# Attention on one core: the softmax's sums over keys moved from TensorE products to VectorE transposes and row sums

## The chip, the cores and the metric

The kernel runs on 1 core of one Trainium2 chip. The metric is the device time of that core in microseconds (us), the median of several runs.

## The reference

`x` holds 32 items of 512 rows by 512 features, `adj` is a 512x512 matrix of zeros and ones. Each item goes through two layers. The first is masked attention with 8 heads of 64 features, an addition of the input and a normalization of the rows; the second is a graph convolution, again with an addition and a normalization.

```python
q = (x @ Wq + bq).reshape(b, n, H, HD)      # k, v in the same way
scores = einsum('bihd,bjhd->bhij', q, k) / sqrt(HD) + mask   # mask: -1e9 where adj == 0
weights = softmax(scores, axis=-1)
x = layernorm(x + einsum('bhij,bjhd->bihd', weights, v).reshape(b, n, H*HD))
deg = adj.sum(axis=1)
norm_adj = adj * deg**-0.5 * deg**-0.5 (rows, columns)
x = layernorm(x + norm_adj @ (x @ weight) + bias)
```

What matters here is the denominator of the softmax: for each item, head and query the sum over 512 keys of exp(score).

## The kernel before, in words

**Layout.** Scores are made transposed: keys on the 128 partitions (4 tiles of keys), queries along the free dimension. One block is two heads of one item; there are 4 blocks an item (`ORDER` is 0, 2, 1, 3) and 128 in all (`blocks`). The exponentials of a block are four tiles `e` of 128x1024, one for each tile of keys, with the two heads side by side.

**The sums.** GpSimd adds the four `e` tiles of a block up into one tile `acc` (`accumulate`; its pool has 2 buffers). Then 128 keys on partitions are left to be summed. `sums(b, c)` does that on TensorE: four products with a 128x32 selector `sel`, one for each head of two blocks, into the four column groups of one PSUM tile. The result goes to `sT` by a copy on ScalarE (c = 0) or an addition on VectorE (c = 1). `finish(b).inverse` turns `sT` with four 128x128 transposes on TensorE, so that queries are on partitions, and takes reciprocals into `inv`. `add` multiplies the attention's result `yT` by `inv`.

**The order of the work is written out by hand.** Every engine takes its instructions in program order (`InOrder` pins it); no planner moves anything. The loop over k has one step for a block. In step k: what is left of the pending additions to `acc` is issued, then come `scores` for the first two key tiles of block k, `values` (the product with V) for block k-1, on every even k one call of `sums`, then `scores` for the last two key tiles. After that comes a share of "side" work: projections of the next item and the second half of the item before, with short pieces on other engines woven in (`beside`). `put_off` (`more`) issues one pending addition to `acc` on GpSimd.

For items 1 to 29 the four steps of an item are always alike. They are called here A (k mod 4 = 1), B (2), C (3) and D (0, the next item's first block). A share has 8 pieces of TensorE work of 1.7 to 1.9 us each:

- A: v0 to v6, the seven products for the next item's values (Strassen's scheme, `values_of`), and k0, the first of the keys and queries. `inverse` comes behind v5, `add` behind v6 and k0.
- B: k1 to k6, l0, l1 (keys and queries); the statistics, roots and `norm` of the first layer come between.
- C: l2, l3, l4, the four products `first` of the convolution, l5.
- D: l6 and the seven products `second` of the convolution.

**Buffers.** All these pieces, `sums` and `inverse` take PSUM tiles from the pool `ps_mm`, which has 3 buffers in turn: a piece starts only when the piece three before it has been read out. Scores have a pool of their own, `ps_sc`, with 2.

**The value pieces.** In `seven`, the piece v3 makes `u2` with `middle` (two additions: the product, then the bias `bv_r`), and v4 is read out by two VectorE instructions of which the first reads `u2`.

**judge** (three small VectorE instructions) checks that the inverses are in a safe range; it stands in B's share behind the last `split`.

Of the kernel before, what the change touches and what calls it, by code (L numbers as in the profile page):

```python
# [9 lines left out]
F32 = mybir.dt.float32  # L10
# [4 lines left out]
ALU = mybir.AluOpType  # L15
AX = mybir.AxisListType

P = 128
H = 8
# [30 lines left out]
def unshifted(  # L50
# [29 lines left out]
    B, N, D = x.shape  # L80
    NT = N // P
# [3 lines left out]
    tensor, vector, scalar, gpsimd = (InOrder(tc, e) for e in (nc.tensor, nc.vector, nc.scalar, nc.gpsimd))  # L85

    consts = ctx.enter_context(tc.tile_pool(name="consts", bufs=1))
    acts = ctx.enter_context(tc.tile_pool(name="acts", bufs=2))
    work = ctx.enter_context(tc.tile_pool(name="work", bufs=2))
    small = ctx.enter_context(tc.tile_pool(name="small", bufs=3))  # L90
# [10 lines left out]
    HALF = N // 2  # L101
# [77 lines left out]
    bv_r = load_row(bv, "bv_r", nc.scalar)  # L179
# [21 lines left out]
    gpsimd.memset(sel, 0.0)  # L201
    for c in range(2):
        gpsimd.memset(sel[:, c, c : c + 1], 1.0)
    FINE = consts.tile([P, B], F32, name="fine")
    maskT = consts.tile([P, NT, N], U8, name="maskT")
    adjT = consts.tile([P, NT, N], F32R, name="adjT")
# [74 lines left out]
    def values_of(b):  # L281


        def multiply(p, i, j):
            for r in range(2):
                for u in range(2):
                    tensor.matmul(
                        p[:, r, :], XT[:, j, u, ts(r, P)], wv[:, i, u, :],
                        start=u == 0, stop=u == 1,
                    )  # L290

        def first(e1, p):
            V[b] = acts.tile([P, NT, D], F32, name="v")
            vector.tensor_add(e1, p, bv_r[:, None, :HALF].to_broadcast([P, 2, HALF]))

        def middle(u2, u1, p):
            vector.tensor_add(u2, u1, p)
            vector.tensor_add(u2, u2, bv_r[:, None, HALF:].to_broadcast([P, 2, HALF]))

        def out(i, j):  # L300
            return V[b][:, 2 * j : 2 * j + 2, ts(i, HALF)]

        return seven(multiply, first, middle, out)
# [70 lines left out]
    def values(s):  # L374
# [27 lines left out]
        for q in range(4):  # L402
# [3 lines left out]
                yb[32 * q : 32 * (q + 1)],  # L406
            )

    def sums(b, c):


        p = ps_mm.tile([P, N], F32, name="mm")
        for q in range(4):
            parts = ACC[b, ORDER[2 * c + q // 2]]
            for k, a in enumerate(parts):
                tensor.matmul(
                    p[32 * q : 32 * (q + 1), :], sel[:, c, :], a[:, q % 2, :],
                    start=k == 0, stop=k == len(parts) - 1,
                )
        if c == 0:  # L420
            SM[b] = work.tile([P, N], F32, name="sT", bufs=1)
            if b < B - 1:
                scalar.copy(SM[b], p)
            else:
                vector.tensor_scalar(SM[b], p, 1e-36, None, op0=ALU.max)
        else:
            vector.scalar_tensor_tensor(SM[b], p, 1e-36, SM[b], op0=ALU.max, op1=ALU.add)

# [21 lines left out]
    def finish(b):  # L450


        t = {}

        def inverse(cs):
            sT = SM[b]
            p = ps_mm.tile([P, NT, 2, 2, 32], F32, name="mm")
            for i in range(NT):
                tensor.transpose(p[:, i].rearrange("p a k r -> p (a k r)"), sT[:, ts(i, P)], ident)
            if cs[0] == 0:  # L460
                t["inv"] = small.tile([P, NT, H], F32, name="inv")
            inv = t["inv"].rearrange("p i (a c k) -> p i a c k", a=2, c=2)
            for c in cs:
                vector.reciprocal(inv[:, :, :, c], p[:, :, :, :, c])

        def judge():

            inv = t["inv"].rearrange("p i h -> p (i h)")
            low = small.tile([P, NT * H], F32, name="low")
            vector.tensor_scalar(low, inv, INV_LOW, None, op0=ALU.is_gt)  # L470
            vector.scalar_tensor_tensor(low, inv, INV_HIGH, low, op0=ALU.is_lt, op1=ALU.mult)
            vector.tensor_reduce(FINE[:, b : b + 1], low, AX.X, ALU.add)

        def add(i):
            y = YT[b][:, i, :]
            vector.tensor_mul(
                y.rearrange("p (h d) -> p h d", h=H), y.rearrange("p (h d) -> p h d", h=H),
                t["inv"][:, i, :, None].to_broadcast([P, H, HD]),
            )
            gpsimd.tensor_add(y, y, R[b][i])  # L480

        def add_pair(i, g):

            y, r = YT[b][:, i, :], R[b][i]
            for h in (2 * g, 2 * g + 1):
                at = slice(h * HD, (h + 1) * HD)
                vector.scalar_tensor_tensor(
                    y[:, at], y[:, at], t["inv"][:, i, h : h + 1], r[:, at], op0=ALU.mult, op1=ALU.add
                )

        def measure(i):
            if i == 0:
                t["mv"] = small.tile([P, NT, 2], F32, name="mv")
            statistics(YT[b][:, i, :], t["mv"][:, i, :])

        def root(i=0, k=NT):
            rstd, add = roots(t["mv"][:, i : i + k], None)
            for n in range(k):
                t["rstd", i + n], t["add", i + n] = rstd[:, n : n + 1], add[:, n : n + 1]

        def norm(i):
            if i == 0:
                if b < B - 1:
                    HI[b], LO[b] = (acts.tile([P, NT, D], F32R, name=k, bufs=1) for k in ("hi", "lo"))
                    LO[b] = [LO[b][:, k, :] for k in range(NT)]
                else:
                    HI[b] = acts.tile([P, NT, D], F32R, name="hi2", tag="v")
                    lo = [acts.tile([P, 2, D], F32R, name="lo2", tag="kq", bufs=5) for _ in range(2)]
                    LO[b] = [lo[k // 2][:, k % 2, :] for k in range(NT)]
            x1 = YT[b][:, i, :]  # L510
            rstd, add = t["rstd", i], t["add", i]
            if b == B - 1 and i % 2:
                vector.tensor_scalar(x1, x1, rstd, add, op0=ALU.mult, op1=ALU.add)
            else:
                scalar.activation(x1, x1, AF.Identity, bias=add, scale=rstd)

            scalar.activation(HI[b][:, i, :], x1, AF.Copy, scale=dis[:, i : i + 1])

        def split(i):
            x1 = YT[b][:, i, :]  # L520
            vector.scalar_tensor_tensor(
                LO[b][i], x1, dis[:, i : i + 1], HI[b][:, i, :], op0=ALU.mult, op1=ALU.subtract
            )
            gpsimd.tensor_add(x1, x1, b1_r)

        def grow(i):
            x1 = YT[b][:, i, :]
            scalar.activation(x1, x1, AF.Copy, scale=rdeg[:, i : i + 1])

        def block(f):  # L530
            return [(0, f, (i,)) for i in range(NT)]

        return dict(
            early=[(0.6, inverse, ((0,),))], late=[(0.6, inverse, ((1,),))],
            pairs=[[(0, add_pair, (i, g)) for i in range(NT)] for g in ORDER],
            halves=[(0, root, (0, 2)), (0, root, (2, 2))],
            inverse=[(0.6, inverse, ((0, 1),))], add=block(add), measure=block(measure), root=[(0, root, ())],
            judge=[(0, judge, ())], norm=block(norm), split=block(split), grow=block(grow),
        )

# [156 lines left out]
    def cut(pieces, counts):  # L697

        lists = [[]]
        left = list(counts)  # L700
        for piece in pieces:
            if piece[0] > 1:
                if not left[0]:
                    left.pop(0)
                    lists.append([])
                left[0] -= 1
            lists[-1].append(piece)
        return lists
# [10 lines left out]
    S = len(blocks)  # L719
# [20 lines left out]
    for k in range(S + 1):  # L740
        b, at = divmod(k, G)
        if at == 1:
# [8 lines left out]
            if b == 0:  # L751
                w1_parts = [(0, weigh_part, (w1, gpsimd, i)) for i in range(4)]
                side = main[:7] + [(0, degrees, ())] + weave(w1_parts, main[7:]) + turn0 + kq[5:] + turn1
                shares = cut(side, (6, 5, 5, 5))
            elif b < B - 1:
                f, c = finish(b - 1), convolve(b - 1)
                norm, split, grow = f["norm"], f["split"], f["grow"]
# [6 lines left out]
                    5: rest[5:6] + f["inverse"], 6: rest[6:] + add[:2], 7: add[2:],  # L764
                    8: measure[:2] + put_off, 9: measure[2:], 10: f["root"] + put_off, 11: norm[:1],
                    12: norm[1:2] + split[:1], 13: norm[2:3] + split[1:2], 14: norm[3:] + split[2:3],
                    15: split[3:] + f["judge"], 16: put_off + grow[:2], 17: put_off + grow[2:], 18: turn0,
                }
                side = sum(([piece] + beside.get(i, []) for i, piece in enumerate(main)), [])
                side += c["first"] + c["parts"] + kq[5:] + turn1[:1]  # L770
# [26 lines left out]
            load_residual(B - 1)  # L797
        if k < S:
            scores((*blocks[k], 0))
        if k:  # L800
            values((*blocks[k - 1], 0))
            if k == S:
                sums(B - 1, 1)
            values((*blocks[k - 1], 1))
            if k % 2 == 0 and k < S:
                sums(blocks[k - 1][0], (k - 1) % G // 2)
        if k < S:
            accumulate((*blocks[k], 0))
# [324 lines left out]
```

## Time and profile before

| | |
|---|---|
| time, median of 3 runs | 2931.66 us (2931.45 to 2931.84) |
| span of the profiled execution | 2929.5 us, granted TensorE clock 0.995 |
| busy TensorE (PE) | 2874.0 us |
| busy VectorE (DVE) | 2081.8 us |
| busy GpSimd (POOL) | 1813.3 us |
| busy ScalarE (ACT) | 1059.1 us |
| chain of waits, by engine | PE 74%, DVE 16%, ACT 6% |
| products with `sel` on `acc` | 504 matmul records, 68.0 us busy |
| transposes of `sT` | 132 records, 19.9 us busy |
| `acc` additions on POOL | 374 of 128x1024, mean 2.36 to 2.41 us |

A matmul in float32 leaves several records. Busy times of an engine count overlapping instructions once. The profile's names follow the program's: `acc`, `sT`, `inv`, `u` for `u2`, `mm` for a tile of `ps_mm`, `sc` for one of `ps_sc`. Since every instruction is issued through the helper `InOrder`, all have its line (L44), and groups are told apart by tiles.

### The profile page before, as it was taken

The numbers are of one execution on the slowest core, as the hardware profiler recorded it, in microseconds if no ns is written. First come the engines' busy times: TensorE is split into PE (matmuls) and PEld (weight loads), VectorE is DVE, ScalarE is ACT, GpSimd is POOL, SyncE is SP. The second block draws the span as 40 slices with busy tenths as digits, with TensorE's granted clock in tenths as the row PEclk, the third lists the DMA queues.
The fourth block names the chain that finished last, engine by engine and source line by source line (L and its number), as shares of the span: only waits on it lengthen the run. The fifth ranks groups of instructions, "written<-read, shape, count | busy, mean of one in ns | idle before, by whom it ended". The sixth has DMA issues, their size and how long they took to land.

```text
span 2929.5 us, 35536 instructions
## 1 busy us (share of the span) xinstructions
PE 2874.0 (98%) x12966; PEld 1885.9 (64%) x12966; DVE 2081.8 (71%) x2926; ACT 1059.1 (36%) x1343; POOL 1813.3 (62%) x1139
## 2 busy tenths in 40 slices
PE   7999999999999999999999999999999999999997
PEld 5666666666666666666666666666666666666655
DVE  6677766677666777666776667776677766677677
ACT  1233333343333433333433334333333333343343
POOL 2566666656666666666666666666666666656665
PEclk9999999999999999999999999999999999999998
DMA  5111122112221121211122211122211122112211
GB/s 130 33 26 47 47 58 51 38 39 51 54 54 41 39 51 47 57 41 40 47 50 55 55 40 36 49 53 54 44 40 47 47 58 54 40 35 49 54 36 52
DMA packets 383401, 142.42 MB, mean 49 GB/s; under 512 B 280049, under 2 KB 349681, under 8 KB 383217
## 3 DMA queue, kind: packets, MB, share of 16 engines
q1 hardware_dynamic: 380720, 138.35, 19.8%
q10 hardware_dynamic: 2496, 1.70, 0.3%
q8 instruction: 104, 1.70, 0.2%
q14 instruction: 81, 0.66, 0.1%
HBM read 72.88 MB, written 33.55 MB: 36 GB/s over the span
## 4 chain that ended last, share of the span: by engine, by line
PE 74%; DVE 16%; ACT 6%; issue 2%; POOL 1%; DMA 0%; SPq 0%; DVEq 0%; POOLq 0%
PE mm L44 47%; PE sc L44 15%; PE av L44 12%; DVE u L44 3%; ACT yT L44 3%; DVE e L44 3%; DVE st L44 3%; ACT hi L44 2%; DVE lo L44 2%; DVE low L44 2%; POOL rstd L44 1%; ACT e L44 1%; DVE mv L44 1%; DVE kq L44 1%; DVE v L44 1%
## 5 line engine op out<-in xcount | busy, mean ns | idle before, releaser
L44 ACT ACTIVATE e<-e 128x1024 f32<-128x1024 f32 x512 | 540.6, 1057 | 1095.1 <-DVE e L44 1076.3
L44 DVE SCALAR_TENSOR_TENSOR e<-sc,maskT 128x1024 f32<-128x1024 f32 x512 | 600.3, 1213 | 83.1 <-PE sc L44 82.7
L44 POOL TENSOR_TENSOR acc<-acc,e 128x1024 f32<-128x1024 f32 x248 | 597.4, 2409 | 64.2 <-ACT e L44 54.4
L44 POOL TENSOR_TENSOR acc<-e 128x1024 f32<-128x1024 f32 x126 | 296.9, 2356 | 382.5 <-ACT e L44 271.4
L44 PE MATMUL sc<-kq 64*128 64x512 f32 x2048 | 518.9, 620 | 14.5 <-DVE e L44 14.5
L44 PE MATMUL mm<-xT,wk 128*128 128x256 f32 x1792 | 469.8, 385 | 1.0 <-DVE off L44 1.0
L44 PE MATMUL av<-e,v 128*64 128x512 f32 x2048 | 467.9, 599 | 0.0
L44 PE MATMUL mm<-xT,wq 128*128 128x256 f32 x1792 | 459.9, 379 | 0.0
L44 PE MATMUL mm<-wv,xT 128*128 128x256 f32 x1792 | 407.2, 385 | 18.2 <-DVE xT L44 11.7
L44 PEld LDWEIGHTS mm<-xT,wk 128*128 128x128 f32 x1792 | 332.7, 190 | 113.4 <-issue 69.7
L44 PEld LDWEIGHTS mm<-wv,xT 128*128 128x128 f32 x1792 | 338.3, 192 | 93.2 <-issue 24.3
L44 PEld LDWEIGHTS mm<-xT,wq 128*128 128x128 f32 x1792 | 340.9, 190 | 45.6
L44 PEld LDWEIGHTS sc<-kq 64*128 64x128 f32 x2048 | 174.2, 186 | 297.9 <-issue 171.9
L44 PEld LDWEIGHTS av<-e,v 128*64 128x64 f32 x2048 | 135.5, 136 | 316.2 <-issue 315.4
L44 DVE TENSOR_TENSOR kq<-u,mm 128x512 f32<-128x512 f32 x128 | 88.0, 688 | 238.0 <-PE mm L44 237.9
L44 POOL TENSOR_TENSOR yT<-yT,xr 128x512 f32<-128x512 f32 x124 | 193.6, 1590 | 80.5 <-DVE yT L44 80.5
L44 POOL TENSOR_TENSOR rstd<-ve,minus_half 128x4 f32<-128x4 f32 (+1 forms) x66 | 66.2, 1003 | 259.3 <-DVE nmu L44 259.3
L44 PE MATMUL mm<-w,zT 128*128 128x256 f32 x992 | 224.6, 379 | 0.0
L44 POOL TENSOR_TENSOR yT<-yT,b_r 128x512 f32<-128x512 f32 x124 | 171.2, 1391 | 56.4 <-DVE lo L44 56.4
L44 PEld LDWEIGHTS mm<-w,zT 128*128 128x128 f32 x992 | 188.4, 190 | 26.8 <-issue 1.5
L44 PE MATMUL mm<-adjT,hi 128*128 128x512 f32 x496 | 203.7, 411 | 0.0
L44 PE MATMUL mm<-adjT,lo 128*128 128x512 f32 x496 | 198.3, 400 | 5.2 <-DVE lo L44 5.2
(124 smaller groups left out, 3178.6 us busy)
## 6 DMA issues: line engine op xcount, KB each, us to landing
x<-in_x_dram SPq DMA_DIRECT2D x256, 128.0 KB, 2.9
out_dram<-y SPq DMA_DIRECT2D x127, 256.0 KB, 2.1
xr<-in_x_dram SPq DMA_DIRECT2D x124, 256.0 KB, 3.5
yT<-yb SPq DMA_DIRECT2D x496, 64.0 KB, 2.5
wv<-in_L_gnn_Wv_dram ACTq DMA_DIRECT2D x8, 128.0 KB, 4.5
wk<-in_L_gnn_Wk_dram SPq DMA_DIRECT2D x8, 128.0 KB, 4.3
wq<-in_L_gnn_Wq_dram SPq DMA_DIRECT2D x8, 128.0 KB, 4.5
yT<-in_adj_dram SPq DMA_DIRECT2D x1, 1024.0 KB, 6.6
```

The lines of the kernel that those rows point to most:

```text
L44: return self.tc.keep_in_program_order(op(*args, **kwargs))
```

## The change

For all items but the last, `fold(b, g)` takes the place of `sums`. It stands in step k behind the first pair of scores and ahead of `values`, for block k-1. It transposes `acc` in place on VectorE in blocks of 32x32 (one 128x1024 instruction), and sums each row over groups of 32 (one instruction, 128x1024 to 128x32) into a tile `folded` that gathers all 8 heads of the item. What is left is to add up, for each of 32 rows, the four groups of 32 partitions: `inverse_all` does it with one product of `folded` (128x128) with a constant `spread`, four small VectorE instructions that clamp and reorder the result, and one reciprocal.

Three more edits go along. The addition of `bv_r` to `u2` in the value pieces moves from VectorE to GpSimd. `judge` moves from B's share to C's, behind l4 and a transpose of x. For the first item, two calls of `more` are put into each share, so that `acc` is complete before `fold` wants it. The last item keeps `sums`, with `sT` in an old weight's buffer.

```diff
+    spread = consts.tile([P, 4, 32], F32, name="spread")
+    vector.tensor_reduce(spread[:, 0], ident.rearrange("p (q r) -> p r q", r=32), AX.X, ALU.add)
+    for q in range(1, 4):
+        gpsimd.tensor_copy(spread[:, q], spread[:, 0])
...
         def middle(u2, u1, p):
             vector.tensor_add(u2, u1, p)
-            vector.tensor_add(u2, u2, bv_r[:, None, HALF:].to_broadcast([P, 2, HALF]))
+            gpsimd.tensor_add(u2, u2, bv_r[:, None, HALF:].to_broadcast([P, 2, HALF]))
...
+    def fold(b, g):
+        a = ACC.pop((b, g))[0]
+        if g == ORDER[0]:
+            SM[b] = small.tile([P, H, N // 32], F32, name="folded")
+        vector.transpose(a.rearrange("p k n -> p (k n)"), a.rearrange("p k n -> p (k n)"))
+        vector.tensor_reduce(
+            SM[b][:, 2 * g : 2 * g + 2].rearrange("p k t -> p (k t)"),
+            a.rearrange("p k (t s) -> p (k t) s", s=32), AX.X, ALU.add,
+        )
...
         if c == 0:
-            SM[b] = work.tile([P, N], F32, name="sT", bufs=1)
-            if b < B - 1:
-                scalar.copy(SM[b], p)
-            else:
-                vector.tensor_scalar(SM[b], p, 1e-36, None, op0=ALU.max)
+            SM[b] = wq[:, 6].rearrange("p u n -> p (u n)")
+            vector.tensor_scalar(SM[b], p, 1e-36, None, op0=ALU.max)
...
+        def inverse_all():
+            p = ps_mm.tile([P, H, NT, 4], F32, name="mm")
+            tensor.matmul(
+                p.rearrange("p h i l -> p (h i l)"), spread.rearrange("p q r -> p (q r)"),
+                SM[b].rearrange("p h t -> p (h t)"), start=True, stop=True,
+            )
+            t["inv"] = small.tile([P, NT, H], F32, name="inv")
+            for l in range(4):
+                at = slice(32 * l, 32 * (l + 1))
+                vector.tensor_scalar(
+                    t["inv"][at].rearrange("p i h -> p h i"), p[at, :, :, l], 1e-36, None, op0=ALU.max
+                )
+            vector.reciprocal(t["inv"], t["inv"])
...
-            inverse=[(0.6, inverse, ((0, 1),))], add=block(add), measure=block(measure), root=[(0, root, ())],
+            inverse=[(0.6, inverse_all, ())], add=block(add), measure=block(measure), root=[(0, root, ())],
...
                 shares = cut(side, (6, 5, 5, 5))
+                for share in shares:
+                    share[1:1] = [(0, more, ())]
+                    share[4:4] = [(0, more, ())]
...
-                    15: split[3:] + f["judge"], 16: put_off + grow[:2], 17: put_off + grow[2:], 18: turn0,
+                    15: split[3:], 16: put_off + grow[:2], 17: put_off + grow[2:], 18: turn0 + f["judge"],
...
             scores((*blocks[k], 0))
+        if k and blocks[k - 1][0] < B - 1:
+            fold(*blocks[k - 1])
         if k:
             values((*blocks[k - 1], 0))
...
-            if k % 2 == 0 and k < S:
+            if k == S - 2:
                 sums(blocks[k - 1][0], (k - 1) % G // 2)
```

## The prediction, made before the changed kernel ran

> **What bounds the kernel now.** First the busy times of the page:
>
> ```profile
> PE 2874.0 (98%) x12966; PEld 1885.9 (64%) x12966; DVE 2081.8 (71%) x2926; ACT 1059.1 (36%) x1343; POOL 1813.3 (62%) x1139
> ```
>
> TensorE (PE) is busy for all but 55 of 2929.5 us, so what leaves PE shortens the kernel, unless a wait takes its place. Next, the busy times by step for one item (A, B, C, D):
>
> ```profile
> 1392.60:1414.88 22.28, 22.11 (x102) 14.94 (x101) 17.53 (x29) 7.16 (x8) 11.49 (x9) 1.00 0.33 102
> 1414.88:1437.30 22.42, 22.42 (x105) 14.68 (x104) 19.63 (x29) 10.62 (x16) 15.89 (x11) 1.00 0.08 12
> 1437.30:1460.01 22.71, 22.33 (x98) 14.38 (x97) 13.16 (x17) 10.49 (x15) 12.67 (x8) 1.00 0.18 35
> 1460.01:1482.43 22.42, 22.42 (x105) 14.68 (x104) 13.57 (x17) 4.81 (x5) 16.46 (x11) 1.00 0.19 40
> ```
>
> After the length come PE, weight loads, VectorE (DVE), ScalarE (ACT), GpSimd (POOL). An item takes 89.83 us. DVE has 2.8 us to spare in B, 4.8 in A, 9.6 in C, 8.9 in D. The timeline of PE shows what goes and the two places where PE already waits for DVE:
>
> ```profile
> 1410.48 0.60 PE L44 MATMUL mm<-ident,sT 128*128 128x128 f32 x4
> 1411.26 1.96 PE L44 MATMUL mm<-wv,xT 128*128 128x256 f32 x8 [0.17 <-DVE e L44]
> ...
> 1420.38 1.06 PE L44 MATMUL mm<-acc,sel 128*32 128x512 f32 x8
> 1421.37 1.99 PE L44 MATMUL sc<-kq 64*128 64x512 f32 x8
> ...
> 1443.25 2.26 PE L44 MATMUL sc<-kq 64*128 64x512 f32 x8 [0.38 <-DVE e L44]
> ```
>
> One call of sums holds PE for 1421.37 - 1420.38 = 0.99 us; the four transposes with the wait behind them for 1411.26 - 1410.48 = 0.78. That first wait is v6's, for the buffer of v4. The timeline of all engines shows its cause:
>
> ```profile
> 1405.40 0.16 DVE L44 TENSOR_SCALAR nmu<-mv 128x4 f32<-128x4 f32 x1
> ...
> 1405.56 1.02 POOL L44 TENSOR_TENSOR rstd<-ve,minus_half 128x4 f32<-128x4 f32 x1 [4.92 <-DVE nmu L44]
> ...
> 1406.80 5.14 POOL L44 TENSOR_TENSOR acc<-acc,e 128x1024 f32<-128x1024 f32 x2
> ...
> 1407.23 0.69 DVE L44 TENSOR_TENSOR u<-e,mm 128x512 f32<-128x512 f32 x1 [1.04 <-PE mm L44]
> ...
> 1407.95 1.77 DVE L44 TENSOR_TENSOR u<-u,bv_r 128x512 f32<-128x512 f32 x1
> 1409.82 0.69 DVE L44 TENSOR_TENSOR v<-u,mm 128x512 f32<-128x512 f32 x1
> ...
> 1410.43 0.68 DVE L44 TENSOR_TENSOR e<-e,mm 128x512 f32<-128x512 f32 x1
> ```
>
> v4's buffer is free when the last of these ends (1411.11). Last, the tiles view for durations (min/median/max in ns):
>
> ```profile
> L44 DVE STREAM_TRANSPOSE xT<-x x64: 1235/1239/1246, 8.3 to 2728.5; 128x1024 f32<-128x1024 f32 x64
> ...
> L44 DVE TENSOR_TENSOR u<-u,bv_r x32: 694/1770/2018, 26.5 to 2755.2; 128x512 f32<-128x512 f32 x32
> ```
>
> **What the skill says.** The Trainium skill, "SBUF — State Buffer", Who interferes with whom: a DVE instruction with two SBUF inputs and a GpSimd one that reads SBUF exclude each other for a whole instruction; one SBUF input or a row reduction doesn't contend. The trace agrees: u<-u,bv_r takes 694 ns at least and 1770 in the median beside acc additions, while the transposes of x stay within 11 ns. "VectorE: DVE Perf Modes", The perf-mode tier table, gives row reductions one element a cycle; the trace has 686 ns for 512 elements and 2280 for 2048. "TensorE: Matmul & The Clock Gate", Part 3, says that small products in different parts of the array overlap; the trace agrees: sums' four 512-column products take 0.99 us, so less goes than their count suggests.
>
> **The change part by part.** Per steady item, in offsets from the start of a step.
>
> PE: two calls of sums go (-1.98 us). The four transposes become one product of 128 columns: half of a 256-column one (8 records in 1.73 us make 4 products, 0.43 each), so 0.22; without any wait that is 0.78 - 0.22 = -0.56. Over 62 calls of sums and 31 inverses: 61.4 + 17.4 = 79 us, the most that can be won.
>
> DVE: each fold is a transpose (1.24) and a reduction of 1024 elements, 1.22 between the two rows above; the second reads the first, so 2.45 with the gap. Four an item: +9.8 us; off go one sT addition (0.69) and u+bv (1.77), and inverse_all takes some 0.9 in place of 0.36. The sT copy on ACT (0.57) goes too. DVE then has about 71.7 us of work in 87.3 of PE. The sum fits; where it stands decides.
>
> A: the first score readouts end at 4.45. Fold runs to 6.9, transposing av to 7.6, the second score readouts to 9.95 (before 9.04). Gaps of 1.17, 0.34, 0.42 and 0.22 us swallow most of it, and nmu ends at 13.21 instead of 12.96. u2's product is only ready at 14.6, so u2 ends at 15.3 as before. But now the bias is POOL's, and POOL takes its queue in order: rstd and add from 13.2 to 14.5, one acc addition to 16.85, and only then u2+bv, 1.28 us (the median of yT<-yT,b_r on POOL is 1276 ns, its maximum 1727), to 18.13. Behind this wait DVE holds both readouts of v4, which end at 19.5, and v6 starts at 19.65. PE is free for it at 18.1: a wait of 1.5 us. A is 19.65 - 18.66 = 1.0 us longer than before, 23.25.
>
> B: DVE enters as late as before (add ends at 3.6). Score readouts to 5.9, fold to 8.35, av to 9.0, score readouts to 11.3 (before 10.1), k1's readout to 11.95, then statistics and readouts without a gap: k2's is done at 14.1, k3's at 16.5, k4's at 17.9. PE has no sums now and reaches k6 at 16.17, which needs k3's buffer: 0.5 us of wait. B takes 22.42 - 0.99 + 0.5 = 21.93.
>
> C: the last split ends 0.75 later against B's start, and C begins 0.5 earlier: at 4.4 instead of 3.14. judge (1.6 us) is gone from there, so score readouts start at 4.35 instead of 4.68, and most of the 0.38 wait and of a second one inside that row (2.26 instead of 1.99) goes: -0.35, so 22.35. Fold then delays l2's readout to 12.6; the piece that needs its buffer starts at 12.9. judge, behind the transpose of x, lies beside the convolution's products, where DVE waited 6.7 us.
>
> D: -0.99, so 21.43; fold lies in the 2.0 us in which DVE waited for av, and the rest in later gaps.
>
> Sum: 23.25 + 21.93 + 22.35 + 21.43 = 88.96 against 89.83, so -0.9 an item, over 30 items -27. The first item: two sums less (-2), but in step 1 fold waits for two acc additions, which in this trace end at 77.4 on POOL; DVE then does the av transpose and the second score readouts at about 83, and the values' buffers hold PE for about 6 us. Together +4. spread is made while DVE and POOL wait for the first loads (8.3 and 11.0 us): nothing. The tile of sT for the last item changes its place only: nothing. No DMA moves.
>
> Total -23 us on the span of 2929.5; the other runs are within 0.4 us of one another and their median is 2.2 above the span, so 2909 us.
>
> Unknown costs, both ends. Fold: at the least 2.25 (two rows back to back without the gap), at the most 3.5 (if it waited for a POOL addition as u+bv does, +1.05). POOL's u2+bv: 1.26 to 1.73. inverse_all's small ones: 0.16 to 0.25 each, hidden until v6's readout at 21.6. fold's wait for acc: nothing after item 0, since the second addition of a block ends 5 us or more before the next step's fold. I take the medians.
>
> **The rivals.** (1) The main case: PE's gain is mostly given back as waits in A and B. (2) The waits don't come: POOL reaches u2+bv before the acc addition, and B's queue is shorter than reckoned. Then it is the 79 less 4 to 8: 2856 to 2864 us. For it: POOL is at 62%. Against it: the order on POOL is fixed, acc ahead of u2. (3) Slower: fold costs more than its rows. Every us on it delays A by one (through nmu, rstd, acc, u2), B by one (k6) and C by about half: 2.5 an item. The gain of 0.9 is gone from a fold of 2.8 us on; at 3.5 it is 88.96 + 2.6 = 91.6, over 30 items +53, +57 with item 0, so 2989. Against it: the even durations of the transposes of x. For it: B has nearly no slack, and an in-place transpose and 32 short sums in one instruction stand nowhere in this trace. (4) It does as it says but the waits eat all: within 6 us.
>
> **How the numbers follow.** 0.2% is 5.9 us, about what a measurement of this kernel can tell. Main case 0.55, 2882 to 2936, most of it faster; rival 2 0.18; rival 3 0.22; rival 4 0.05. Faster 0.55 x 0.85 + 0.18 = 0.65, same 0.055 + 0.05 = 0.11, slower 0.24. The range takes in rival 2 and the beginning of rival 3: 2860 to 2945.
>
> **What would show it right or wrong.** In the profile after, v6 waits about 1.5 us for DVE with v<-u,mm ended by POOL u; k6 waits about 0.5 for DVE; C's second scores wait less than 0.38; the fold pair takes 2.45 us; an item takes about 88.96 us and A is the one step that grew. If A shrinks, rival 2 holds; if fold takes over 2.8 us, rival 3.

## The result, and the profile after

The changed kernel takes 2891.85 us, the median of 4 runs (2891.36 to 2893.16), against 2931.55 for the kernel before on the same chip: a ratio of 0.9865, 95% interval 0.9848 to 0.9882, or 39.7 us less. The span of the profiled execution went from 2929.5 to 2890.0 us.

The busy times of the page after, to be held against the same line of before:

```profile
PE 2813.2 (97%) x12408; PEld 1867.5 (65%) x12408; DVE 2292.3 (79%) x3205; ACT 1041.4 (36%) x1312; POOL 1844.5 (64%) x1174
```

TensorE lost 61 us of busy time, VectorE got 210 and GpSimd 31 more. PE's unused time grew from 55 to 77 us: about a third of the busy time taken off PE came back as unused time. The four steps of one item (after the length: PE, weight loads, VectorE, ScalarE, GpSimd; then the granted clock) show where:

```profile
1287.90:1310.79 22.89, 21.88 (x99) 14.81 (x99) 18.65 (x33) 7.16 (x8) 12.33 (x10) 1.00 0.32 99
1310.79:1332.53 21.74, 21.69 (x97) 14.43 (x96) 20.46 (x30) 8.91 (x12) 15.29 (x10) 1.00 0.09 13
1332.53:1354.85 22.32, 22.32 (x98) 14.37 (x97) 16.36 (x20) 11.62 (x17) 13.03 (x9) 1.00 0.17 36
1354.85:1376.28 21.43, 21.43 (x98) 14.51 (x97) 15.16 (x18) 4.81 (x5) 16.80 (x11) 1.00 0.21 41
```

A is the one step that grew, by 0.61 us, and there PE is 1.01 us less busy than the step is long. D lost its 0.99 us of sums and nothing else. Items 2 to 29 repeat this within 0.1 us (in item 1, A took 22.52). The timeline of PE after has the places at which it waits (a bracket at the end of a row is the idle time before it and what ended it):

```profile
1305.78 0.39 PE L44 MATMUL mm<-folded,spread 128*128 128x128 f32 x2
1307.17 1.97 PE L44 MATMUL mm<-wv,xT 128*128 128x256 f32 x8 [1.01 <-DVE e L44]
...
1326.08 1.03 PE L44 MATMUL mm<-xT,wq 128*128 128x256 f32 x4
1327.16 1.13 PE L44 MATMUL mm<-xT,wk 128*128 128x256 f32 x4
...
1338.09 2.26 PE L44 MATMUL sc<-kq 64*128 64x512 f32 x8
```

v6 starts 1.01 us after PE was free. In B, k6 (the row at 1327.16) comes 1.08 us behind the row before it where its neighbours come after 0.86 or 0.87, so it is held for 0.2 though no bracket says so (a matmul's end is modelled). C's second scores have lost their bracket of 0.38; the row is still 2.26 us long, so the short wait inside it stayed. The timeline of GpSimd after shows why v6 waits,

```profile
1300.86 1.02 POOL L44 TENSOR_TENSOR rstd<-ve,minus_half 128x4 f32<-128x4 f32 x1 [4.92 <-DVE nmu L44]
1301.95 0.20 POOL L44 TENSOR_TENSOR add<-nmu,rstd 128x4 f32<-128x4 f32 x1
1302.11 2.37 POOL L44 TENSOR_TENSOR acc<-acc,e 128x1024 f32<-128x1024 f32 x1
1304.43 1.27 POOL L44 TENSOR_TENSOR u<-u,bv_r 128x512 f32<-128x512 f32 x1
1305.66 2.35 POOL L44 TENSOR_TENSOR acc<-acc,e 128x1024 f32<-128x1024 f32 x1
```

and that of VectorE after shows fold in its place and the wait that came with it:

```profile
1292.27 1.24 DVE L44 STREAM_TRANSPOSE acc<-acc 128x1024 f32<-128x1024 f32 x1
1293.54 1.22 DVE L44 TENSOR_REDUCE folded<-acc 128x32 f32<-128x1024 f32 x1
1294.67 0.71 DVE L44 STREAM_TRANSPOSE yb<-av 128x512 f32<-128x512 f32 x1
...
1302.53 0.69 DVE L44 TENSOR_TENSOR u<-e,mm 128x512 f32<-128x512 f32 x1 [1.04 <-PE mm L44]
1305.74 0.69 DVE L44 TENSOR_TENSOR v<-u,mm 128x512 f32<-128x512 f32 x1 [2.52 <-POOL u L44]
```

u2 is there at 1303.2, but its bias waits until 1304.43 behind rstd and an acc addition. VectorE sits for 2.52 us, in every item: the list of waits has "DVE v <- POOL u" with 75.9 us in 31 times.

The last place is step 1, once, in the timeline of all engines after:

```profile
76.46 1.25 DVE L44 STREAM_TRANSPOSE acc<-acc 128x1024 f32<-128x1024 f32 x1 [7.87 <-POOL acc L44]
...
82.57 8.08 PE L44 MATMUL mm<-wv,xT 128*128 128x256 f32 x24 [5.31 <-DVE e L44]
```

The first fold waits 7.87 us for acc, and PE then waits 5.31 us for a buffer. PE's 24 records behind that wait take 8.08 us; the 24 ahead of it take 5.45. The busy times of the stretch from 81.14 us on show why, in the granted clock of 0.50:

```profile
81.14:87.97 6.83, 5.40 (x13) 4.36 (x14) 3.34 (x5) 1.76 (x2) 5.56 (x3) 0.50 0.27 37
```

So step 1, which grew from 18.66 to 26.46 us, lost 5.3 us to the wait and some 2.5 to the clock behind it.

### The profile page after: what moved, and what is told of

Same layout as the page of the kernel before. It is cut to its first block, busy times and chain, and to the rows that moved or that the text cites. A ratio compares the mean times of both kernels' runs of the same rounds, so it can differ in the third digit from the quotient of the medians.

```text
span 2890.0 us, 34431 instructions
## 1 busy us (share of the span) xinstructions
PE 2813.2 (97%) x12408; PEld 1867.5 (65%) x12408; DVE 2292.3 (79%) x3205; ACT 1041.4 (36%) x1312; POOL 1844.5 (64%) x1174
## 4 chain that ended last, share of the span: by engine, by line
PE 81%; DVE 11%; POOL 3%; ACT 2%; issue 1%; DMA 0%; SPq 0%; DVEq 0%; POOLq 0%
PE mm L44 49%; PE sc L44 17%; PE av L44 16%; DVE e L44 3%; DVE st L44 2%; ACT y L44 2%; DVE v L44 1%; POOL u L44 1%; POOL rstd L44 1%; DVE mv L44 1%; DVE u L44 1%; DVE yb L44 0%; DVE kq L44 0%; DMA x<-in_x_dram 0%; DVE lo L44 0%
## 5 line engine op out<-in xcount | busy, mean ns | idle before, releaser
L44 POOL TENSOR_TENSOR acc<-acc,e 128x1024 f32<-128x1024 f32 x248 | 588.5, 2373 | 187.3 <-ACT e L44 182.5
```

The lines of the kernel that those rows point to most:

```text
L44: return self.tc.keep_in_program_order(op(*args, **kwargs))
```

## The experiments

Two theories stood against each other. "Places": PE has lost time at a few places only, each set by the order of one queue (v6 behind GpSimd's queue in A, k6 behind VectorE's in B, step 1). "Load": VectorE's 210 us of new work hold PE up wherever they stand. The table has what every run gave; the steps are medians over items 1 to 29 of each trace, from the first scores of a step to those of the next, and the times medians.

| kernel | A | B | C | D | item | time | ratio to before (95% interval) |
|---|---|---|---|---|---|---|---|
| before | 22.28 | 22.43 | 22.69 | 22.43 | 89.81 | 2931.6 | |
| forecast | 23.25 | 21.93 | 22.35 | 21.43 | 88.96 | 2909 | |
| changed | 22.90 | 21.74 | 22.31 | 21.43 | 88.38 | 2891.9 | 0.9865 (0.9848 to 0.9882) |
| bias on VectorE | 22.28 | 21.74 | 22.31 | 21.43 | 87.77 | 2875.3 | 0.9808 (0.9791 to 0.9824) |
| bias first | 21.75 | 22.29 | 22.31 | 21.43 | 87.78 | 2875.2 | 0.9805 (0.9789 to 0.9822) |
| judge back | 22.89 | 21.75 | 23.92 | 21.43 | 89.99 | 2949.0 | 1.0060 (1.0044 to 1.0077) |
| reduction twice | 23.98 | 23.00 | 23.20 | 21.43 | 91.61 | 3006.9 | 1.0254 (1.0237 to 1.0271) |
| no fold | 22.90 | 21.43 | 21.98 | 21.43 | 87.74 | 2865.5 | 0.9773 (0.9757 to 0.9789) |
| first fold later | 22.89 | 21.74 | 22.31 | 21.43 | 88.37 | 2887.1 | 0.9847 (0.9831 to 0.9863) |
| acc apart | 21.75 | 24.28 | 22.31 | 21.43 | 89.78 | 2935.4 | 1.0014 (1.0007 to 1.0021) |
| four places | 21.75 | 21.43 | 21.98 | 21.43 | 86.59 | 2835.1 | 0.9671 (0.9655 to 0.9687) |

**Bias on VectorE.**

```diff
-            gpsimd.tensor_add(u2, u2, bv_r[:, None, HALF:].to_broadcast([P, 2, HALF]))
+            vector.tensor_add(u2, u2, bv_r[:, None, HALF:].to_broadcast([P, 2, HALF]))
```

> The changed kernel (2891.9 us) with one edit undone: the bias bv_r is added to u2 on VectorE again. Theory 'places' (PE loses at a few places only, the largest being v6 in step A, which waits because u2's bias stands behind an acc addition in GpSimd's queue): VectorE's addition waits for that same acc addition (it ended at offset 16.53) and ends at 17.1 instead of 17.76, so A shortens by 0.65 us, 30 items: about 2872 us. Theory 'load' (VectorE's 210 us of added work is what holds PE, wherever it stands): 32 more VectorE instructions of 1.8 us make it slower, 2895 to 2910 us.

A shortened to 22.28 and no other step moved, though VectorE's busy time rose to 2346.3 us. So this edit of the change, which takes 54 us of work off VectorE, costs 17 us. More load, less time: a first blow to "load".

**Bias first.**

```diff
-  0: rest[:1], 1: rest[1:3], 2: put_off, 3: rest[3:4], 4: rest[4:5] + put_off,
+  0: rest[:1], 1: rest[1:3], 3: rest[3:4] + put_off, 4: rest[4:5] + put_off,
```

> The changed kernel with the first acc addition of step A issued behind v3 instead of ahead of it, so that GpSimd reaches u2's bias first. No engine's work changes. 'Places': u2's bias ends at offset 16.6 instead of 17.76, v6 starts at about 18.1, its wait of 1.0 us vanishes, A takes 21.75 us instead of 22.89: about 2858 us. 'Load': no change, 2886 to 2898 us.

A came out at 21.75 as "places" has it, and PE has no wait left there. Half of the gain was lost again in B, which neither theory had. GpSimd's timeline of this run has the two acc additions together now,

```profile
1297.82 1.27 POOL L44 TENSOR_TENSOR u<-u,bv_r 128x512 f32<-128x512 f32 x1 [1.14 <-DVE u L44]
1299.05 4.80 POOL L44 TENSOR_TENSOR acc<-acc,e 128x1024 f32<-128x1024 f32 x2
```

and VectorE's timeline has the multiplications by inv beside the end of the second:

```profile
1303.16 5.18 DVE L44 TENSOR_TENSOR yT<-yT,inv 128x512 f32<-128x512 f32 x4
```

They took 4.64 us in the changed kernel. The first of them makes the difference:

```profile
1303.16 1.23 DVE L44 TENSOR_TENSOR yT<-yT,inv 128x512 f32<-128x512 f32 x1
```

It took 0.68 us in the changed kernel; here it ends 0.55 us behind the GpSimd addition that runs (1299.05 + 4.80 = 1303.85). Both read two tensors from SBUF, so this fits the exclusion that the prediction quoted. VectorE enters B 0.54 us later, and B gets 0.55 longer. That the late entry makes B longer is read off the timeline; no run tests it alone.

**Judge back.**

```diff
-  15: split[3:], ... 18: turn0 + f["judge"],
+  15: split[3:] + f["judge"], ... 18: turn0,
```

> The changed kernel with judge at the end of step B's share again. 'Places': it lies between the last split and C's score readouts, as before the change; these come 1.3 to 1.6 us later and C's second scores wait 1.2 us longer, C takes 23.5 us instead of 22.3: about 2928 us, which would be most of the change's gain. 'Load': VectorE's work is the same, and C has 6 us of idle VectorE time: 2886 to 2898 us.

C grew by 1.61 us, judge's own length at that place (1361.11 to 1362.73 in one item), and in 5 of 29 items by 1.65 more (see the last section): 30 x 1.61 + 5 x 1.65 = 57 us, which is the measured difference of 57.1. VectorE's work is the same (busy for 2299 us against 2292), so "load" cannot explain this. Three instructions in the wrong place would have turned the change's 40 us of gain into a loss of 17.

**The reduction twice.**

```diff
         vector.tensor_reduce(
             SM[b][:, 2 * g : 2 * g + 2].rearrange("p k t -> p (k t)"),
             a.rearrange("p k (t s) -> p (k t) s", s=32), AX.X, ALU.add,
         )
+        vector.tensor_reduce(
+            SM[b][:, 2 * g : 2 * g + 2].rearrange("p k t -> p (k t)"),
+            a.rearrange("p k (t s) -> p (k t) s", s=32), AX.X, ALU.add,
+        )
```

> The changed kernel with fold's row sum done twice (the second writes the same sums again), so every fold is longer by one reduction of 1.13 us. 'Places': delays A and B by 1.1 each and C by 0.5 to 0.9, D by nothing: 2.7 to 3.2 us an item, 2972 to 2990 us. 'Load': VectorE would be busy for 2434 us; if its load is what binds, all 124 x 1.13 = 140 us come on top, 3032 us. If fold were hidden altogether: 2892 us.

A +1.08, B +1.26, C +0.89, D nothing: 3.2 us an item for 4 x 1.25 us of added work (1.13 each was expected). The steps are near those of "places", but the time is a miss: 3006.9 us lies above the 2972 to 2990 expected. The steps alone (30 x 3.2 = 97) fall short of the measured 115; the rest is 12 items of 29 in which A took a further 1.7 us (last section). This is also the price of rival 3: a fold longer by a microsecond costs 2.6 us an item.

**No fold.**

```diff
+    same = consts.tile([P, 32], F32, name="same")
+    gpsimd.memset(same, 1.0)
...
-        vector.transpose(a.rearrange("p k n -> p (k n)"), a.rearrange("p k n -> p (k n)"))
         vector.tensor_reduce(
-            SM[b][:, 2 * g : 2 * g + 2].rearrange("p k t -> p (k t)"),
-            a.rearrange("p k (t s) -> p (k t) s", s=32), AX.X, ALU.add,
+            SM[b][:, 2 * g : 2 * g + 2].rearrange("p k t -> p (k t)"), same[:, :, None], AX.X, ALU.add
         )
```

> The changed kernel without fold's work: the 32x32 transposes and the row sums are left out, and 'folded' is filled with ones by a 32-element instruction (so the softmax isn't divided by its sums). 'Places': A keeps the wait of v6, since nmu and the acc addition ahead of u2's bias come as before (22.85 us); k6's wait in B goes (21.43), C loses its wait of 0.27 and a little more (22.0), D stays (21.43); step 1 doesn't wait for acc (-7): 87.7 us an item, about 2865 us, so that fold itself costs some 27 of its 297 us of VectorE time. 'Load': all waits go with the work, 2853 us, the time before less the 79 us of TensorE work removed.

A is unchanged to 0.01 us with fold's work gone: in A, fold at its present length costs nothing, and all of A's loss belongs to GpSimd's queue. There is little to spare, though: 1.25 us more of it cost A 1.08 in "reduction twice". B and C lose 0.31 and 0.33. All of fold costs 26 us, step 1 included.

**First fold later.**

```diff
-        if k and blocks[k - 1][0] < B - 1:
+        if k == 2:
+            fold(*blocks[0])
+        if k > 1 and blocks[k - 1][0] < B - 1:
             fold(*blocks[k - 1])
```

> The changed kernel with the very first fold put into step 2 instead of step 1, so that it doesn't wait for GpSimd's two acc additions. Step 1 took 33.75 us against 26.65 before the change; if the fold's wait made all of that, about 7 us go: 2885 us. If GpSimd's addition of u2's bias or something else in step 1 made it: 2889 to 2892 us.

Step 1 went from 26.46 to 18.66 us, which is what it took before the change, so the fold's wait, with the slow clock behind it, made all of its growth. (The 33.75 and 26.65 of the expectation are steps 0 and 1 together.) Step 2, with two folds, took 18.64 instead of 16.25: of the 7.8 won, 2.4 were given back one step later. Step 0, up to which the kernels are alike, took 0.9 us longer in this run; between all runs it varies from 7.3 to 8.3.

**Acc apart.**

```diff
-  0: rest[:1], 1: rest[1:3], 2: put_off, 3: rest[3:4], 4: rest[4:5] + put_off,
-  5: rest[5:6] + f["inverse"], 6: rest[6:] + add[:2], 7: add[2:],
+  0: rest[:1], 1: rest[1:3], 3: rest[3:4] + put_off, 4: rest[4:5],
+  5: rest[5:6] + f["inverse"], 6: rest[6:] + add[:2], 7: add[2:] + put_off,
```

> As e2, but of A's two pending acc additions one comes behind v3 and the other behind the last 'add' piece, so that only one lies ahead of the multiplication of yT on VectorE. In e2, A was 1.15 us shorter, but B 0.55 longer: yT's four multiplications took 5.18 instead of 4.64 us beside the second acc addition, and VectorE entered B later. If that collision made B longer, B is back at 21.74 us and A stays at 21.75: 87.2 us an item, about 2857 us. If it was A's being shorter in itself: 2875 us as e2.

A miss: B grew to 24.28. The collision was gone (the multiplications took 4.6 us from first to last, and VectorE entered B 3.63 us into it as in the changed kernel, not 4.17 as in "bias first"), but the moved addition is one that the next fold needs. GpSimd's timeline of this run,

```profile
1328.80 6.25 POOL L44 TENSOR_TENSOR yT<-yT,xr 128x512 f32<-128x512 f32 x4 [2.51 <-DVE yT L44]
1335.01 2.36 POOL L44 TENSOR_TENSOR acc<-acc,e 128x1024 f32<-128x1024 f32 x1
```

and VectorE's:

```profile
1337.40 1.25 DVE L44 STREAM_TRANSPOSE acc<-acc 128x1024 f32<-128x1024 f32 x1 [2.46 <-POOL acc L44]
```

Behind yT's four additions the acc addition ends at 1337.4; B's fold waits 2.46 us for it, and the scores' second readouts stand behind the fold. The expectation had overlooked that fold folds the block of the step before.

**Four places.** Acc apart and first fold later, and besides:

```diff
-  12: norm[1:2] + split[:1], 13: norm[2:3] + split[1:2], 14: norm[3:] + split[2:3],
+  12: norm[1:2] + split[:1], 13: norm[2:3] + split[1:2], 14: norm[3:] + split[2:3] + [(0, fold, (b, ORDER[1]))],
...
-        if k > 1 and blocks[k - 1][0] < B - 1:
+        if k > 1 and blocks[k - 1][0] < B - 1 and (b == 0 or at != 2):
             fold(*blocks[k - 1])
```

> e6 and e7 together, and A's block folded at the end of B, behind the third split, instead of at B's beginning, so that the readouts k1 to k3 come earlier. VectorE's work is that of the changed kernel. 'Places': A 21.75, B 21.43 (no wait), C 22.05, D 21.43, 86.66 us an item, which is what TensorE has to do: about 2833 us. 'Load': not under e7.

2835.1 us, the fastest of all, 96 us under the kernel before and 57 under the changed one with the same instructions in another order. "Load" is out with it. The new places were not run one by one; fold at the end of B is known from this run only. The busy times by step have PE busy from end to end of the item (first number behind the length):

```profile
1174.52:1196.27 21.75, 21.75 (x100) 14.81 (x99) 18.72 (x33) 7.16 (x8) 10.05 (x9) 1.00 0.35 105
1196.27:1217.70 21.43, 21.43 (x98) 14.51 (x97) 19.70 (x29) 10.15 (x15) 18.18 (x12) 1.00 0.09 13
1217.70:1239.68 21.98, 21.98 (x98) 14.44 (x97) 16.53 (x21) 10.36 (x15) 12.68 (x8) 1.00 0.17 37
1239.68:1261.11 21.43, 21.43 (x98) 14.51 (x97) 15.15 (x18) 4.81 (x5) 16.49 (x11) 1.00 0.20 40
```

## Why the prediction was right, and where a size was off

The direction, what bounds the kernel and the places of the waits (v6 in A, k6 in B, step 1) were forecast rightly, and the runs bear them out. The gain was 39.7 us and not 23, because the first two of these waits were sized too large. In two smaller terms, C and the first item, the sum came out close partly by luck.

- **What leaves PE.** 0.99 us for a call of sums: D went from 22.43 to 21.43. The new inverse product: 0.22 reckoned; in "bias first", where nothing waits behind it, v6 follows after 0.25.
- **Fold's price.** 2.45 reckoned. The two rows have means of 1231 and 1220 ns, and fold holds VectorE for 1294.67 - 1292.27 = 2.40 us. What the prediction quoted from the Trainium skill ("SBUF — State Buffer", Who interferes with whom) holds for these two: 1225 to 1245 and 1219 to 1222 ns from least to most, beside a GpSimd that is busy for 64% of the time. Rival 3's ground is gone. It does not hold for every instruction with one SBUF input, and the page excepts some modes, which the prediction left out: judge's first instruction has one and took 975 ns in the median, 175 at the least, and in each of items 1 to 29 it ended 0.04 us behind an acc addition.
- **A, the larger mis-sized term.** "A is 1.0 us longer" was 0.61. The wait reckoned at 1.5 us shows as 1.01 in the bracket; without it A is 1.15 shorter ("bias first"). The chain is the one forecast (nmu, rstd, add, acc, u2's bias, v4's readouts, v6), but each link came early, in offsets from A's start: nmu at 12.96 instead of 13.21, u2's bias at 17.80 instead of 18.13, v6 at 19.27 instead of 19.65. Durations had been laid end to end, while an engine starts its next instruction before the last one's row ends: two score readouts take 2.33 us, not twice 1.207; the acc addition has 2.37 us and the next begins after 2.32. Of the 0.38 us by which v6 came early, 0.25 arose ahead of nmu: fold was to push nmu back by that much, but it vanished in VectorE's gaps, and "no fold" confirms that fold adds nothing to A.
- **B, the smaller one.** k6's wait was to be 0.5 and was 0.31 (21.74 against 21.43, which "no fold" and "four places" show to be B without a wait), for the same reason: k3's readout was to be done 16.5 us into B and was at 16.3.
- **C.** -0.35 forecast, -0.38 measured, but made up otherwise: the wait of 0.38 went whole, and the one inside the row, of which most was to go, stayed (2.26 us still). judge's move makes 1.6 us of difference ("judge back").
- **The first item.** +4 forecast, +5.1 measured. Step 1 took 7.8 us more: PE's wait, reckoned at about 6, was 5.3, and the slow clock behind it, some 2.5, stood in no term. The two sums went (-2), and step 0 happened to be 0.7 shorter.

The sum: an item went from 89.81 to 88.38, so 1.43 and not 0.87; over 30 items that is the 17 us by which the forecast fell short. Rival 2 (no waits) did not come: A's wait is real. But it comes from the place that the change gave to u2's bias: putting the bias back on VectorE takes 0.62 of its 1.15 us away, issuing it ahead of the acc addition takes all, though B then loses 0.55. Rival 2's range has a slip (79 less 4 to 8 ends at about 2861 us, not 2864), and 79 us, "the most that can be won", was too low: "four places" wins 96, since the two waits that C had before, 0.65 us an item, go too.

Not tried: other places for fold in C and D, where "no fold" shows no more than 0.33 us an item to be had.

## What to carry to other kernels

Moving work from a full engine to one with room pays what the full engine loses, less what each moved instruction delays behind it in its new queue; read that off step by step, because the sum of busy times (here 210 us more on VectorE, and 40 us less in all) does not show it. Handing a short instruction to a less busy engine can cost more than it takes away when that engine works in order: ask what stands ahead of it, not how busy the engine is. Before moving an addition later, look for its reader: the wait moves to whoever needs it next.

## What the runs showed of the hardware that was not expected

Waits of PE of 1.6 us and more cost extra now and then. In "judge back" C's second scores wait 1.6 us in every item, but in 5 of 29 items the step is 1.65 us longer still. Busy times of that run: an ordinary C, a long one, and two stretches of the long one; the third number from the end is the granted clock of TensorE:

```profile
633.53:657.46 23.93, 22.34 (x97) 14.37 (x96) 16.59 (x20) 11.61 (x17) 13.28 (x9) 1.00 0.17 33
723.54:749.10 25.56, 23.97 (x98) 15.06 (x97) 16.60 (x20) 11.71 (x17) 13.24 (x9) 0.93 0.16 31
728.72:732.13 3.41, 1.82 (x8) 0.60 (x8) 3.38 (x5) 1.38 (x2) 0.53 (x1) 1.00 0.00 0
732.13:735.54 3.41, 3.41 (x9) 1.59 (x6) 3.38 (x4) 0.74 (x1) 2.35 (x1) 0.50 0.00 0
```

PE's timeline of the long one shows the wait and the slow matmuls behind it:

```profile
730.70 2.96 PE L44 MATMUL sc<-kq 64*128 64x512 f32 x8 [1.59 <-DVE e L44]
733.59 2.07 PE L44 MATMUL mm<-xT,wk 128*128 128x256 f32 x4
```

The second row takes 1.13 us in an ordinary item. A stretch of 3.41 us at half the clock loses 1.7 us of full clock, which is about what the step grew by.

The trace shows where such a stretch can begin. In "judge back" the five begin at 732.13, 1093.94, 1725.41, 2356.87 and 2718.69 us; the distances between them are 106, 185, 185 and 106 times 3.413 us. In "reduction twice" the twelve lie 27 or 81 times 3.413 us apart. So both runs fit a fixed grid of windows of 3.413 us, and it is the window behind the one with the wait that runs at half the clock. Counted by these windows:

- "reduction twice", items 2 to 29, A's wait of 2.1 us: all 12 waits that lie in one window were followed by a slow one, none of the 16 that are split over two.
- "judge back", C's wait of 1.6 us: 16 lie in one window, and 5 of them were followed by a slow one, those that began 0.20 to 0.47 us into it; none of the 13 split ones was.
- The changed kernel, A's wait of 1.0 us: none in items 1 to 29. In its one long wait, the 5.3 us of step 1, the clock fell to half for 6.83 us.

Idle time in the window doesn't decide alone: 1.72 us of it ("reduction twice") was not followed by a slow window, and 1.59 ("judge back") was. What decides near 1.6 us stays open, also because the ends of matmuls are modelled. The Trainium skill, "TensorE: Matmul & The Clock Gate", Part 1, tells of a gate that halves the clock after an idle window of about 3.4 us, with windows that run freely. The trace agrees on the windows. It differs on the idle one: PE was busy for 1.82 of the 3.41 us from 728.72 on, and the clock was halved all the same.
